# First layer norm of a fused attention and feed-forward block in two token halves, products of zeros ahead of its transposes, Newton steps on GpSimd, and other load and output orders

## The chip, the core and the metric

The kernel runs on one core of a Trainium2 chip. The metric is the device time of one launch in microseconds (us); the time given for a kernel is the median of its runs. Beside the timed runs there is one execution recorded by the hardware profiler, in which every instruction of TensorE (PE; its weight loads are PEld), VectorE (DVE), ScalarE (ACT), GpSimd (POOL) and the DMA queues (SP's above all) has a start and a duration. L12 means line 12 of the kernel file, and lines without a remark are those of the kernel before.

## The reference

x is 16 x 512 x 512 in float32: 16 batches of 512 tokens. Both branches read the same normalised input and are added to x:

```
xn  = (x - mean(x)) / sqrt(var(x) + 1e-5)                # over the last axis
q, k, v = split(xn @ w_qkv.T + b_qkv)                    # 16 heads of 32
att = softmax(causal(q @ k.T / sqrt(32))) @ v
out = x + (att @ w_out.T + b_out)
        + ((silu(xn @ gate_w.T * gate_s) * (xn @ up_w.T * up_s)) @ down_w.T) * down_s   # 512 -> 1408 -> 512
```

gate_w, up_w and down_w hold only -1, 0 and 1.

## The kernel before

**Arithmetic.** Products run in f16. A float32 operand is split into a high half (a cast, mostly on ACT) and a low half (the difference from it, on DVE or POOL), and a product of two such operands is three products: high by high, low by high, high by low. So the 128 x 512 result of a projection with 512 inner elements is twelve matmuls (`mm_group`: four blocks kc of 128 rows, three pairs). The projections' weights wq are staged in float32 and split by `split_wqkv` into wq_h on ACT and wq_l on DVE or, for the first 128 columns of q and of k, in two steps on POOL (L369, L373). The feed-forward weights fit in fp8 exactly, and are loaded as such by GpSimd's DMAs (`load_ffn`, L405; names wg, wu, wd).

**Tiles and loops.** A batch is four token tiles tb of 128 tokens. Its 16 heads are four groups g; batch and group make 64 slots, taken two at a time by `attention_pair`. In a slot PE makes scores s, DVE adds the mask and takes the row maximum (L668), ACT takes the exponential p (L673) and, scaled, pq (L700, and L705 on DVE), a DMA transposes pq to pT, and PE forms av from pT and v. The rest of PE's work (q and k projections `qk_proj` with their copies qkt, qkh, qkl; v; the feed-forward products g, u and dn with ft, hh and hl between them; the output projection op) fills the room between.

**Layer norm.** `ln_load` brings the four x tiles of a batch to xc; `ln_stats` takes mean and variance per token on DVE (L475, L476) and, once for all four tiles, 1/sqrt by two integer operations and three Newton steps of three DVE operations each on 128 x 4 values (`newton_rsqrt`, L33 to L38). `ln_norm` normalises xc (L493). In batches 1 to 15 `ln_turn` casts the result and DMAs transpose it (xnh, xnl to xh, xl). In batch 0 there is no time for this: two tiles are normalised on ACT (L1106, with the shift of L1096) and two on DVE, PE transposes them in sixteen float32 transposes (`ln_tr`, L523) into four PSUM tiles lnT, one per block kc, which ACT casts to xh (L528) and DVE subtracts to xl (L531). The first products of q and k follow.

**Order.** Nothing is issued as the program text has it. Every operation is recorded as a step of `Plan` with its engine, an estimated duration, what it reads and writes, and a slack. `layout` is a list scheduler that lays the steps out by these estimates: on PE by the steps' keys (their places in time, which `Fill.place` gives out; a step may overtake others within AHEAD), on the other engines by the latest time `late` at which a step may start, found backwards from the pass before. `order(6)` makes six passes and takes the shortest. Each engine then executes its instructions in exactly that order (one queue an engine; POOL's and SP's DMA issues lie in the same queues). PSUM and work tiles come from rings (`Tile` with a tag and a number of buffers), and the first user of a buffer waits for the last of the one before. So an edit of one step's engine or estimate also moves steps far from it.

**The start.** x of batch 0 is loaded first, then wq in six pieces: the two pieces of the first 128 columns, the others, and v's two. The planner chooses their order on SP; in the profile a 768 KB piece goes first, and bqk comes after them. `load_ffn` has 35 pieces in all, each waiting for the one two ahead; the first waits for the token "first", which is written with the low halves qkl of group 0.

**The end.** Three quarters of the last batch's output projection are done early (`out_tile` with `upto`), and the rest in two parts, `more`: two products with oh (high half of the attention output) and one with ol. The calls come in this order:

```
for tb in (0, 1, 0, 1, 2, 2, 3, 3):
    ends[tb](f)
```

y is then formed on DVE (L914) and sent out by SP.

## Time and profile before

| | |
|---|---|
| median of 3 timed runs | 1875.51 us (1872.38 to 1876.12) |
| profiled execution | 1874.57 us, of which the span from first to last instruction is 1872.7 us |
| mean clock granted to TensorE | 0.998 of full |
| busy: PE, DVE, ACT, POOL | 1840.9, 1582.0, 1410.6, 966.5 us |
| DMA | 268.94 MB, 144 GB/s |

Busy time is an engine's own work; a step whose operand is not ready holds up all that stands behind it on its engine. In a timeline line the columns are start, busy time, engine, line, operation, output and inputs, shape, how many instructions lie in the group, and in brackets how long the engine was idle ahead of it and what it waited for; a group of matmuls is as long as from its first start to its last end, so that several can overlap. In the view of waits a line says who waited for what: sum in us, times, and the longest. In the windows view the columns are the stretch, its length, each engine's busy time with its instructions, PE's clock, and the DMA engines' share and rate.

### The profile page before, as it was taken

What the parts mean: (1) busy time and instruction counts of PE and PEld (TensorE: products, weight loads), DVE (VectorE), ACT (ScalarE), POOL (GpSimd) and SP (SyncE); (2) the same over time, 40 slices, a digit from 0 to 9 for tenths busy, and PEclk for the clock granted to TensorE, in tenths of its full rate; (3) what the DMA queues carried; (4) which work ended last, traced back from release to release, by engine and by line L of the source; (5) the groups of instructions that cost most, each with busy time, mean ns of one, the idle gap of its engine ahead of it and who ended that gap; (6) DMA issues with size and microseconds to landing.
All of it is one profiled execution on the core that took longest, in us unless ns stands there. A gap on an engine that the chain in (4) does not pass through costs nothing.

```text
span 1872.7 us, 41104 instructions
## 1 busy us (share of the span) xinstructions
PE 1840.9 (98%) x14994; PEld 872.6 (47%) x14994; DVE 1582.0 (84%) x3791; ACT 1410.6 (75%) x3310; POOL 966.5 (52%) x741
## 2 busy tenths in 40 slices
PE   7999999999999999999999999999999999999998
PEld 3444444444444444444444444444444444444443
DVE  6879889889898888979789797897988979787877
ACT  6676877778777787777778777787777877778774
POOL 4654563645645455464645636456363563645543
PEclk9999999999999999999999999999999999999999
DMA  7888676778767688677776867968678786767766
GB/s 163 122 153 168 111 161 142 138 149 144 152 136 143 143 147 154 133 162 135 140 164 129 162 134 127 175 125 164 131 132 167 137 154 128 145 138 140 129 137 131
DMA packets 842545, 268.94 MB, mean 144 GB/s; under 512 B 806496, under 2 KB 813024, under 8 KB 842336
## 3 DMA queue, kind: packets, MB, share of 16 engines
q1 hardware_dynamic: 837296, 264.08, 73.2%
q0 software_dynamic: 5040, 2.16, 1.7%
q8 instruction: 119, 1.95, 0.4%
q14 instruction: 90, 0.74, 0.1%
HBM read 55.59 MB, written 16.78 MB: 39 GB/s over the span
## 4 chain that ended last, share of the span: by engine, by line
PE 85%; DVE 6%; ACT 3%; DMA 2%; POOL 2%; issue 1%; SPq 0%; POOLq 0%; DVEq 0%; ACTq 0%
PE dn L338 15%; PE qk L338 15%; PE u L338 14%; PE g L338 13%; PE op L338 9%; PE v L338 8%; PE s L629 6%; PE av L770 5%; DVE pq L705 2%; ACT p L673 2%; DVE s L668 1%; DMA xl<-xnl 1%; DVE xc L493 1%; POOL xnl L507 1%; DVE ft L860 0%
## 5 line engine op out<-in xcount | busy, mean ns | idle before, releaser
L673 ACT ACTIVATE p<-s,negm 128x512 f32<-128x512 f32 (+3 forms) x1024 | 529.2, 527 | 220.5 <-DVE negm L668 219.2
L668 DVE CUSTOM_DVE_ANT_0 s<-s,mask 128x512 f32<-128x512 f32 (+3 forms) x1024 | 476.5, 515 | 126.2 <-PE s L629 114.4
L705 DVE SCALAR_TENSOR_TENSOR pq<-p,pq 128x1024 f16<-128x1024 f32 (+1 forms) x384 | 491.6, 1301 | 19.9 <-ACT pq L700 15.3
L864 POOL TENSOR_TENSOR hl<-ft,hh 128x512 f16<-128x512 f32 x176 | 245.2, 1394 | 307.5 <-ACT hh L863 284.7
L700 ACT ACTIVATE pq<-p 128x1024 f16<-128x1024 f32 (+1 forms) x384 | 342.0, 915 | 2.9
L338 PE MATMUL u<-xh,wu 128*128 128x512 f16 x704 | 267.3, 380 | 3.7 <-DVE ft L854 3.7
L338 PE MATMUL dn<-wd,hh 128*128 128x512 fp8e4 x704 | 267.2, 380 | 1.8 <-DMA wd<-in_wdT 1.8
L338 PE MATMUL g<-xh,wg 128*128 128x512 f16 x704 | 267.0, 379 | 0.0
L338 PE MATMUL dn<-wd,hl 128*128 128x512 fp8e4 x704 | 266.8, 379 | 0.0
L338 PE MATMUL g<-xl,wg 128*128 128x512 f16 x704 | 266.8, 379 | 0.0
L338 PE MATMUL u<-xl,wu 128*128 128x512 f16 x704 | 266.8, 379 | 0.0
L571 POOL TENSOR_TENSOR qkl<-qkt,qkh 128x512 f16<-128x512 f32 x128 | 171.8, 1344 | 145.9 <-ACT qkh L569 144.3
L338 PEld LDWEIGHTS <-wg 128*128 128x128 fp8e4 x1408 | 135.9, 98 | 168.0 <-issue 6.6
L338 PEld LDWEIGHTS <-wu 128*128 128x128 fp8e4 x1408 | 133.2, 98 | 165.3 <-issue 8.5
L673 ACT ACTIVATION_READ_ACCUMULATOR p<-s,negm 128x1 f32 x1024 | 207.9, 203 | 0.0
L792 POOL TENSOR_SCALAR Rs<-Rs,bv_c 128x512 f32<-128x512 f32 x63 | 100.0, 1587 | 117.3 <-DVE Rs L785 117.3
L566 ACT ACTIVATE qkt<-qk,bqk_c 128x512 f32<-128x512 f32 x128 | 88.1, 689 | 93.0 <-PE qk L338 91.4
L338 PEld LDWEIGHTS <-wq_h 128*128 128x128 f16 x1024 | 99.4, 98 | 124.2 <-issue 7.9
L860 DVE SCALAR_TENSOR_TENSOR ft<-u,gu_c,ft 128x512 f32<-128x512 f32 x176 | 132.0, 750 | 26.0 <-PE u L338 13.7
L854 DVE SCALAR_TENSOR_TENSOR ft<-ft,g 128x512 f32<-128x512 f32 x176 | 119.8, 681 | 32.0 <-ACT ft L850 28.4
L668 DVE DVE_READ_ACCUMULATOR2_ANT negm<- 128x1 f32 x1024 | 144.3, 141 | 0.0
L850 ACT ACTIVATE ft<-g,gt_c 128x512 f32<-128x512 f32 x176 | 120.6, 685 | 31.2 <-PE g L338 30.6
(123 smaller groups left out, 3161.9 us busy)
## 6 DMA issues: line engine op xcount, KB each, us to landing
xc<-in_x SPq DMA_DIRECT2D x64, 256.0 KB, 4.3
xr<-in_x SPq DMA_DIRECT2D x64, 256.0 KB, 2.9
out<-y SPq DMA_DIRECT2D x64, 256.0 KB, 2.3
pT<-pq SPq DMA_TRANSPOSE x384, 4.3
exact<-in_wdT SPq DMA_DIRECT2D x11, 256.0 KB, 2.8
exact<-in_wgT SPq DMA_DIRECT2D x8, 256.0 KB, 3.1
exact<-in_wuT SPq DMA_DIRECT2D x8, 256.0 KB, 2.8
wq<-in_wqkvT SPq DMA_DIRECT2D x2, 768.0 KB, 7.8
```

Of the source, the lines that this page charges most:

```text
L338: nc.tensor.matmul(ps(), l, r, start=(first + k == 0), stop=(first + k == n - 1))
L571: "POOL", gps(512), lambda: nc.gpsimd.tensor_tensor(l(), t(), h(), ALU.subtract),
L629: nc.tensor.matmul(pss[j]()[:, off[u] : off[u] + n], q()[rows, i * P : (i + 1) * P], k()[rows, 0:n], start=(x == 0), stop=(x == 2), tile_p ...
L668: nc.vector.tensor_tensor_reduce(sc, sc, mask[:, 512 - n :], -(2.0 ** -7), 3e38, ALU.add, ALU.min, negm()[:, m : m + 1])
L673: nc.scalar.activation(exps(u).rearrange("p (k j) q -> p k j q", j=4)[:, :, j, :], part().rearrange("p (k q) -> p k q", q=P), AF.Exp, bias ...
L700: "ACT", 0.2 + 0.00085 * n, lambda src=src, half=half: nc.scalar.mul(half(0), src(), 2.0 ** 15),
L705: lambda src=src, half=half: nc.vector.scalar_tensor_tensor(half(1), src(), 2.0 ** 15, half(0), ALU.mult, ALU.subtract),
L792: "POOL", gps(n), lambda: nc.gpsimd.tensor_scalar(r(), r(), bias, None, ALU.add),
L850: "ACT", act(512) + 0.1, lambda: nc.scalar.activation(t(), pg(), AF.Tanh, scale=gt_c[:, ic : ic + 1]),
L854: "DVE", dve(512), lambda: nc.vector.scalar_tensor_tensor(t(), t(), 1.0, pg(), ALU.add, ALU.mult),
L860: lambda: nc.vector.scalar_tensor_tensor(t(), pu(), gu_c[:, ic : ic + 1], t(), ALU.mult, ALU.mult),
L864: add("POOL", gps(512), lambda: nc.gpsimd.tensor_tensor(hl(), t(), hh(), ALU.subtract), r=[t, hh], w=[hl])
```

## The change

There are six edits.

1. `first_row` takes the place of `ln_tr` and of batch 0's statistics and norm. Tiles 0 and 1 are half 0, tiles 2 and 3 half 1, each with its own statistics. Half 0 has its seed on DVE and its Newton steps, as well as the shift, on GpSimd (14 operations of 128 x 2); half 1 does all on DVE. ACT normalises tiles 0, 1 and 3, DVE tile 2. PE transposes tile 0 (four blocks), tile 1 (four), then tiles 2 and 3 block by block.
2. `warm_up` puts 42 matmuls of zeros (128 x 128 by 128 x 384, from the mask's zero columns into a PSUM tile nobody reads) ahead of the transposes and six between tile 1's and the others'.
3. In batches 1 to 15 the seed stays on DVE and the three Newton steps become `newton_steps`, twelve operations on GpSimd; the running minimum vmin is a DVE step of its own.
4. The first 128 columns' wq_l come from DVE like the others. The wq loads and those before are forced into the order of the code (`behind`), bqk after the fourth piece; the planner's estimates of loads change (BEGIN, FIRST_TURN, lat). q's and k's first group are recorded in single matmuls (`piece=1`), so that PE alternates between them.
5. `load_ffn` begins once v's first half piece is loaded, and each piece waits for the one three ahead.
6. The last output parts run as (0, 1, 0, 1, 2, 3, 2, 3), each after the one before.

In the order that the planner then gives, PE's instructions are the same ones apart from those in edits 1 and 2, and from about batch 6 on they also stand in nearly the same order.

```diff
...
+def rsqrt_seed(nc, y, v):
+    yi = y.bitcast(I32)
+    nc.vector.tensor_scalar(yi, v.bitcast(I32), 1, None, ALU.logical_shift_right)
+    nc.vector.tensor_scalar(yi, yi, -1, 0x5F3759DF, ALU.mult, ALU.add)
+
+
+def newton_steps(nc, y, v, t):
+
+    for _ in range(3):
+        nc.gpsimd.tensor_tensor(t, v, y, ALU.mult)
+        nc.gpsimd.tensor_tensor(t, t, y, ALU.mult)
+        nc.gpsimd.tensor_scalar(t, t, -0.5, 1.5, ALU.mult, ALU.add)
+        nc.gpsimd.tensor_tensor(y, t, y, ALU.mult)
+
+
 AHEAD = 20.0
 
 SWITCH, LANDING = 0.095, 1.4
 WINDOW = 0.5
+
+BEGIN, FIRST_TURN = 0.75, 1.3
 
 RUNS = 0.0, 0.17, 0.30, 0.64, 0.80
 LAST_RUNS = 0.0, 0.14, 0.28, 0.42, 0.56
...
-        free = dict.fromkeys(self.ENGINES, 0.0)
+        free = dict.fromkeys(self.ENGINES, BEGIN)
         ready = {e: [] for e in self.ENGINES}
-        made, done, dma, mode = {}, [], 0.0, "wide"
+        made, done, dma, mode = {}, [], FIRST_TURN, "wide"
         keys = sorted((s.key, s.n) for s in self.steps if s.eng == "PE")[::-1]
 
         def begin(st):
 
             t, more = st.at, {}
+            if st.behind and st.behind.end is None:
+                return None
             for b in st.tiles:
                 if b.index is None:
                     l = made.setdefault(b.tag, [])
...
         add(
             "SP", 0.5,
             lambda: nc.sync.dma_start(staged(t, kcs)[:, :, cols], src.rearrange("(k p) f -> p k f", p=P)),
-            w=[(t, k)], lat=4.8 * (cols.stop - cols.start) * (kcs.stop - kcs.start) / 2048,
+            w=[(t, k)], lat=1.6 if cols.stop == P else 3.2 * (cols.stop - cols.start) * (kcs.stop - kcs.start) / 2048,
         )
 
     def split_wqkv(part, k, t, cols, kcs=slice(0, KC)):
...
         dst = slice(part * 512 + cols.start, part * 512 + cols.stop)
         h, l = wq_h[:, kcs, dst], wq_l[:, kcs, dst]
         add("ACT", act(n), lambda: nc.scalar.mul(h, staged(t, kcs)[:, :, cols], 256.0), r=[(t, k)], w=[("wqh", part, k)])
-        if cols.stop == P:
-
-            src = lambda: staged(t, kcs)[:, :, cols]
-            add(
-                "POOL", gps(n), lambda: nc.gpsimd.tensor_scalar(src(), src(), 256.0, None, ALU.mult),
-                r=[(t, k), ("wqh", part, k)], w=[(t, k)],
-            )
-            add(
-                "POOL", gps(n), lambda: nc.gpsimd.tensor_tensor(l, src(), h, ALU.subtract),
-                r=[(t, k), ("wqh", part, k)], w=[("wql", part, k)],
-            )
-            return
         add(
             "DVE", dve(n),
             lambda: nc.vector.scalar_tensor_tensor(l, staged(t, kcs)[:, :, cols], 256.0, h, ALU.mult, ALU.subtract),
...
             for kc in range(KC)
             for nm, dst, src in (("wg", wg, wgT), ("wu", wu, wuT))
         ] + [(wd[:, ic, :], wdT[ic * P : (ic + 1) * P, :], ("wd", ic), 512) for ic in range(IC)]
-        before = ["first", "first"]
+        before = [(wst[3], 1)] * 3
         for dst, src, tok, n in pieces:
             add(
                 "POOL", 0.5, lambda dst=dst, src=src: nc.gpsimd.dma_start(dst, src),
-                r=[before[-2]], w=[tok], lat=0.8 * n / 512,
+                r=[before[-3]], w=[tok], lat=0.8 * n / 512,
             ).dma = True
             before.append(tok)
 
...
 
             add("DVE", 0.8, stat, r=[xc], w=[(bs, tb), (mv, tb)], slack=slack)
 
+        def seed():
+
+            nc.vector.tensor_scalar(v(), mv()[:, :, 1], EPS, 2.0 ** -20, ALU.add, ALU.mult)
+            rsqrt_seed(nc, y(), v())
+
         def rstd():
-
-            nc.vector.tensor_scalar(v(), mv()[:, :, 1], EPS, 2.0 ** -20, ALU.add, ALU.mult)
+            newton_steps(nc, y(), v(), t())
+
+        def least():
             nc.vector.tensor_tensor(vmin, vmin, mv()[:, :, 1], ALU.min)
-            newton_rsqrt(nc, y(), v(), t())
-
-        add("DVE", 2.4, rstd, r=[(mv, tb) for tb in range(NT)], w=[v, y, t], slack=slack)
+
+        add("DVE", 0.5, seed, r=[(mv, tb) for tb in range(NT)], w=[v, (y, 0)], slack=slack)
+        add("POOL", 2.9, rstd, r=[(mv, tb) for tb in range(NT)] + [v, (y, 0)], w=[y, t], slack=slack)
+        add("DVE", 0.08, least, r=[(mv, tb) for tb in range(NT)], w=["vmin"], slack=slack)
 
     def ln_norm(b, tb, slack):
         s = st[b]
...
                 r=[half], w=[(dst, tb)], lat=0.8,
             )
 
...
+    def first_row(f):
+
+        s = st[0]
+        xs, xh, xl = s["xs"], s["xh"], s["xl"]
+        pss = [Tile(pp, [P, 512], F32, "s1", 4, f"lnT_{kc}") for kc in range(KC)]
+
+        def turn(tbs, kcs):
+            def tr():
+                for kc in kcs:
+                    for tb in tbs:
+                        nc.tensor.transpose(
+                            pss[kc]()[:, tb * P : (tb + 1) * P], xs[tb]()[:, kc * P : (kc + 1) * P], ident
+                        )
+
+            f.pe(0.214 * len(tbs) * len(kcs), tr, [xs[tb] for tb in tbs], [(pss[kc], tb) for kc in kcs for tb in tbs])
+
+        for half, pool in ((0, True), (1, False)):
+            nm = f"0_{half}"
+            tile = work("ln_" + nm, "ln0", 2, (P, 24))
+            mv = lambda tile=tile: tile()[:, 0:4].rearrange("p (u n) -> p u n", n=2)
+            bs = lambda tile=tile: tile()[:, 4:16].rearrange("p (u n) -> p u n", n=6)
+            v, y, t, shift = ((lambda tile=tile, k=k: tile()[:, k : k + 2]) for k in (16, 18, 20, 22))
+            tok = lambda *names, tile=tile: [(tile, n) for n in names]
+            eng = nc.gpsimd if pool else nc.vector
+            for u in (0, 1):
+
+                def stat(u=u, mv=mv, bs=bs, xc=xs[2 * half + u]):
+                    nc.vector.bn_stats(bs()[:, u, :], xc())
+                    nc.vector.bn_aggr(mv()[:, u, :], bs()[:, u, :])
+
+                add("DVE", 0.8, stat, r=[xs[2 * half + u]], w=tok(u), slack=-8)
+
+            def seed(mv=mv, v=v, y=y, pool=pool):
+                nc.vector.tensor_scalar(v(), mv()[:, :, 1], EPS, 2.0 ** -20, ALU.add, ALU.mult)
+                if pool:
+                    rsqrt_seed(nc, y(), v())
+
+            def rstd(mv=mv, v=v, y=y, t=t, shift=shift, eng=eng, pool=pool, half=half):
+                (newton_steps if pool else newton_rsqrt)(nc, y(), v(), t())
+
+                eng.tensor_tensor(t(), mv()[:, :, 0], y(), ALU.mult)
+                eng.tensor_scalar(shift(), t(), -1.0, None, ALU.mult)
+
+            def least(mv=mv, half=half):
+                nc.vector.tensor_tensor(
+                    vmin[:, 2 * half : 2 * half + 2], vmin[:, 2 * half : 2 * half + 2], mv()[:, :, 1], ALU.min
                 )
 
-        f.pe(0.45, tr, s["xs"], [ps])
-        add("ACT", act(512), lambda: nc.scalar.copy(xh()[:, kc, :], ps()), r=[ps], w=[(xh, kc)], slack=-8)
-        add(
-            "DVE", dve(512),
-            lambda: nc.vector.tensor_tensor(xl()[:, kc, :], ps(), xh()[:, kc, :], ALU.subtract),
-            r=[ps, (xh, kc)], w=[(xl, kc)], slack=-8,
-        )
+            add("DVE", 0.5 if pool else 0.2, lambda fn=seed: fn(), r=tok(0, 1), w=tok("seed"), slack=-8)
+            add(
+                "POOL" if pool else "DVE", 2.9 if pool else 2.6, lambda fn=rstd: fn(), r=tok(0, 1, "seed"),
+                w=tok("y"), slack=-8,
+            )
+            add("DVE", 0.08, lambda fn=least: fn(), r=tok(0, 1), w=["vmin"], slack=5)
+            for u in (0, 1):
+                xc = xs[2 * half + u]
+                if not pool and u == 0:
+                    add(
+                        "DVE", 0.5,
+                        lambda xc=xc, mv=mv, y=y: nc.vector.tensor_scalar(
+                            xc(), xc(), mv()[:, 0, 0:1], y()[:, 0:1], ALU.subtract, ALU.mult
+                        ),
+                        r=[xc] + tok(0, "y"), w=[xc], slack=-8,
+                    )
+                else:
+                    add(
+                        "ACT", act(512) + 0.1,
+                        lambda u=u, xc=xc, shift=shift, y=y: nc.scalar.activation(
+                            xc(), xc(), AF.Identity, bias=shift()[:, u : u + 1], scale=y()[:, u : u + 1]
+                        ),
+                        r=[xc] + tok("y"), w=[xc], slack=-8,
+                    )
+        warm_up(f, 42)
+        turn((0,), range(KC))
+        turn((1,), range(KC))
+        warm_up(f, 6)
+        for kc in range(KC):
+            turn((2, 3), (kc,))
+        for kc, ps in enumerate(pss):
+            toks = [(ps, tb) for tb in range(NT)]
+            add(
+                "ACT", act(512), lambda kc=kc, ps=ps: nc.scalar.copy(xh()[:, kc, :], ps()), r=toks, w=[(xh, kc)],
+                slack=-8,
+            )
+            add(
+                "DVE", dve(512),
+                lambda kc=kc, ps=ps: nc.vector.tensor_tensor(xl()[:, kc, :], ps(), xh()[:, kc, :], ALU.subtract),
+                r=toks + [(xh, kc)], w=[(xl, kc)], slack=-8,
+            )
+
+    warm = Tile(pp, [P, 512], F32, "av", 1, "warm")
+
+    def warm_up(f, n):
+
+
+        def run():
+            for _ in range(n):
+                nc.tensor.matmul(warm()[:, 0:384], mask[:, 0:P], mask[:, 0:384], start=True, stop=True)
+
+        f.pe(1.5 + 0.161 * n if n > 20 else 0.161 * n, run, [], [warm])
 
...
-            late=0 if b or g else 8,
+            late=0 if b or g else 11, piece=4 if b or g else 1,
         )
...
             return finish()
         steps = iter([(0, 2), (2, 3)])
 
-        def more(f):
-
-            nonlocal last
+        def more(f, after):
+
             k0, k1 = next(steps)
-            last = mm_group(f, ps, ops([upto])[k0:k1], first=3 * upto + k0, n=3 * NG, after=last)
+            after = mm_group(f, ps, ops([upto])[k0:k1], first=3 * upto + k0, n=3 * NG, after=last + after)
             if k1 == 3:
                 finish()
+            return after
 
         return more
 
...
     pieces += [(2, k, wst[2 + k], both, slice(2 * k, 2 * k + 2)) for k in range(2)]
     for n, piece in enumerate(pieces):
         load_wqkv(*piece)
-        if n == 1:
+        if n == 3:
             add("SP", 0.5, lambda: nc.sync.dma_start(bqk_c, bqk), w=["bqk"], lat=0.3)
-    ln_stats(0, -8)
-    shift = work("shift", "rden", 2, (P, 16))
-    mv, y = st[0]["mv"], st[0]["ln"][1]
-    add(
-        "DVE", 0.2,
-        lambda: nc.vector.scalar_tensor_tensor(shift()[:, 0:NT], mv()[:, :, 0], -1.0, y(), ALU.mult, ALU.mult),
-        r=[(mv, tb) for tb in range(NT)] + [y], w=[shift], slack=-8,
-    )
-    for tb in range(NT):
-        if tb % 2 == 0:
-            ln_norm(0, tb, -8)
-            continue
-        xc = st[0]["xs"][tb]
-        add(
-            "ACT", act(512),
-            lambda tb=tb, xc=xc: nc.scalar.activation(
-                xc(), xc(), AF.Identity, bias=shift()[:, tb : tb + 1], scale=y()[:, tb : tb + 1]
-            ),
-            r=[xc, shift, y], w=[xc], slack=-8,
-        )
-
+    loads = [step for step in plan.steps if step.dma]
+    for before, step in zip(loads, loads[1:]):
+        step.behind = before
...
     f = Fill()
-    for kc in range(KC):
-        ln_tr(f, 0, kc)
+    first_row(f)
     for which in (0, 1):
         qk_proj(f, 0, 0, which)
     f.place(0.0, f.total)
...
             count_good(when, start - 0.6 * T)
     av_step(NB - 1, NG - 1, start - 0.3 * T)
     f = Fill()
-    for tb in (0, 1, 0, 1, 2, 2, 3, 3):
-        ends[tb](f)
+    after = []
+    for tb in (0, 1, 0, 1, 2, 3, 2, 3):
+        after = ends[tb](f, after)
     f.place(start, f.total)
```

More of the change, by code (lines that the diff above doesn't have):

```diff
@@ L72, in __init__ @@
         self.end = self.late = None
+        self.behind = None
 class Plan:
@@ L464, in ln_load @@
                 "SP", 0.5, lambda tb=tb, xc=xc: nc.sync.dma_start(xc(), x[b, tb * P : (tb + 1) * P, :]),
-                r=when, w=[xc], lat=0.85,
+                r=when, w=[xc], lat=0.85 if b else 1.05,
             )
@@ L513, in ln_turn @@
             )
-    def ln_tr(f, b, kc):
-        s = st[b]
-        ps = Tile(pp, [P, 512], F32, "s1", 4, f"lnT_{b}_{kc}")
-        xh, xl = s["xh"], s["xl"]
-        def tr():
-            for tb in range(NT):
-                nc.tensor.transpose(
-                    ps()[:, tb * P : (tb + 1) * P], s["xs"][tb]()[:, kc * P : (kc + 1) * P], ident
-                )
-        f.pe(0.45, tr, s["xs"], [ps])
-        add("ACT", act(512), lambda: nc.scalar.copy(xh()[:, kc, :], ps()), r=[ps], w=[(xh, kc)], slack=-8)
-        add(
-            "DVE", dve(512),
-            lambda: nc.vector.tensor_tensor(xl()[:, kc, :], ps(), xh()[:, kc, :], ALU.subtract),
-            r=[ps, (xh, kc)], w=[(xl, kc)], slack=-8,
-        )
+    def first_row(f):
[34 more added lines that the diff above has]
+                    vmin[:, 2 * half : 2 * half + 2], vmin[:, 2 * half : 2 * half + 2], mv()[:, :, 1], ALU.min
+                )
+            add("DVE", 0.5 if pool else 0.2, lambda fn=seed: fn(), r=tok(0, 1), w=tok("seed"), slack=-8)
[39 more added lines that the diff above has]
+            )
@@ L1088, in fast_path @@
         load_wqkv(*piece)
-        if n == 1:
+        if n == 3:
             add("SP", 0.5, lambda: nc.sync.dma_start(bqk_c, bqk), w=["bqk"], lat=0.3)
-    ln_stats(0, -8)
-    shift = work("shift", "rden", 2, (P, 16))
-    mv, y = st[0]["mv"], st[0]["ln"][1]
-    add(
-        "DVE", 0.2,
-        lambda: nc.vector.scalar_tensor_tensor(shift()[:, 0:NT], mv()[:, :, 0], -1.0, y(), ALU.mult, ALU.mult),
-        r=[(mv, tb) for tb in range(NT)] + [y], w=[shift], slack=-8,
-    )
-    for tb in range(NT):
-        if tb % 2 == 0:
-            ln_norm(0, tb, -8)
-            continue
-        xc = st[0]["xs"][tb]
-        add(
-            "ACT", act(512),
-            lambda tb=tb, xc=xc: nc.scalar.activation(
-                xc(), xc(), AF.Identity, bias=shift()[:, tb : tb + 1], scale=y()[:, tb : tb + 1]
-            ),
-            r=[xc, shift, y], w=[xc], slack=-8,
-        )
+    loads = [step for step in plan.steps if step.dma]
+    for before, step in zip(loads, loads[1:]):
+        step.behind = before
     def scale_bqk():
```

## The prediction

> **What bounds the kernel now.** I read the engine table of the page first, then the windows view of a long middle stretch.
>
> ```profile
> PE 1840.9 (98%) x14994; PEld 872.6 (47%) x14994; DVE 1582.0 (84%) x3791; ACT 1410.6 (75%) x3310; POOL 966.5 (52%) x741
> 60.00:1800.00 1740.00, 1728.66 (x14172) 819.46 (x14172) 1484.76 (x3545) 1324.78 (x3117) 910.86 (x673) 1.00 0.76 144
> ```
>
> PE is busy 1840.9 of 1872.7 us and holds 99.3% of the middle stretch. The change takes no product away, so it can only win PE's 31.8 idle us, or stretches at a lower clock. Third, the waits on PE:
>
> ```profile
> PE lnT L523 <- DVE xc L493: 11.0, 1, 11.0
> PE u L338 <- DVE ft L854: 3.7, 4, 1.5
> PE s L629 <- ACT p L673: 3.6, 5, 1.0
> PE dn L338 <- DMA wd<-in_wdT: 1.8, 1, 1.8
> PE qk L338 <- POOL wq_l L373: 1.2, 1, 1.2
> ```
>
> Eleven us stand before the first transpose, the rest in single waits; the same view cut to 60 to 170 us has most of those on ft and p and the one on wd. So I read, fourth, the timeline of the start:
>
> ```profile
> 7.62 0.18 DVE L476 BATCH_NORM_AGGREGATE mv<-bs 128x2 f32<-128x6 f32 x1
> 8.45 0.16 DVE L36 SCALAR_TENSOR_TENSOR ln_t<-ln_v,ln_y 128x4 f32<-128x4 f32 x1
> 8.64 0.16 DVE L37 TENSOR_TENSOR ln_t<-ln_t,ln_y 128x4 f32<-128x4 f32 x1
> 10.42 1.52 ACT L1106 ACTIVATE xc<-xc,shift,ln_y 128x512 f32<-128x512 f32 x2 [4.86 <-DVE shift L1096]
> 10.99 4.04 PE L523 MATMUL lnT<-ident,xc 128*128 128x128 f32 x16 [10.99 <-DVE xc L493]
> 14.82 1.64 PE L338 MATMUL qk<-xh,wq_h 128*128 128x512 f16 x4
> 15.06 0.59 ACT L528 CAST xh<-lnT 128x512 f16<-128x512 f32 x1 [0.27 <-PE lnT L523]
> 16.30 1.03 PE L338 MATMUL qk<-xl,wq_h 128*128 128x512 f16 x4
> 21.97 1.04 PE L338 MATMUL qk<-xh,wq_l 128*128 128x512 f16 x4 [1.19 <-POOL wq_l L373]
> 27.16 1.03 PE L338 MATMUL v<-wq_h,xh 128*128 128x512 f16 x4
> ```
>
> The reader is to see the chain (statistics, Newton steps on four columns, norm, transpose, cast, products) and that the first four products take 1.64 us where later ones take 1.03: the clock is low until about 16. The 48 products of q and k end at about 26.95.
>
> **The start, part by part.** The forecast is a chain of rows in the new order. Half 0 needs two of the four statistics: these end at 5.30 by the rows (5.12 and 0.18); three seed steps at the Newton pitch of 0.20 end at 5.9. Then 14 GpSimd operations of 2 columns. No row has one so small. Their bounds: 0.18 each, a memset's 0.10 and the 0.08 that separates the dependent GpSimd pair at 14.15 (1.52 after 12.55); and 0.50, the 0.53 memset of 512 elements almost whole. I take 0.23: 0.15, near a DVE Newton step's 0.16, which with four columns is fixed cost and not elements either, plus the 0.08; and 0.8 once for meeting DVE's instructions. That ends at 5.9 + 3.2 + 0.8 = 9.9. ScalarE meanwhile loads its table (no longer behind x) and makes the first high weights once they land. Norms of x0, x1, x3 on ScalarE at the row's 0.76 pitch end at 10.75, 11.45, 12.2; x2 comes from DVE by 11.6.
>
> The 48 products of zeros are 1/4 shorter than a 512-wide one: 0.75 x 0.216 = 0.162 warm, 0.32 cold. [...] Transposes, 0.213 apart while cold where nothing waits (the sixteen in 4.04), go at half, 0.107. Those of x1 end at 11.9, six more zeros (0.97) at 12.9, and the four turns of x2 and x3 feed casts that end from 14.0 to 15.7, against 15.65 before. So the last cast is not earlier: ACT carries three norms, a weight piece and four casts in a row. The gain lies behind it: the products start warm (4 x 0.21 = 0.8 saved), run q and k in turn, so none waits for a whole row, and the 1.2 wait for wq_l goes because DVE makes it in one step in place of GpSimd's 2.53 and 1.66. Of the 48 products 24 are done by 19.6, and the others, 24 x 0.216 = 5.2, by 24.8: **2.1 us** earlier than 26.95. Next late there is qkt, which ends near 21.6, before v is through.
>
> Bounds: with 0.50 per GpSimd step the chain is 3.8 later, and x2 and x3 wait less than x0, so I count 2.9 of it: 0.8 lost. With 0.18, no interplay and all loads early, 3.5 gained.
>
> [...]
>
> Six feed-forward loads now leave GpSimd right after the values' weights are under way instead of at 27.23: six issues at 0.55 (the L405 rows) lie ahead of GpSimd's first qkl. They land about 0.63 apart before, so 3.8 us of transfer can delay the last wq piece from 15.99 to 19.8; ScalarE reaches it at about 19.8. I count nothing, 1 us if that cover is gone.
>
> **The wait on wd.** All wd issues now stand ahead of group 3's qkl and of all but the first of batch 1's four xnl; before, the last was issued at 110.60 behind an xnl that waited 5.97, and landed at 114.15. The 1.8 us on PE goes; next late would be hl, whose GpSimd rows start at 111.19, hence 1.0 to 2.0: **1.8**.
>
> **Newton steps of batch 1.** Here they decide something:
>
> ```profile
> 59.54 1.15 POOL L571 TENSOR_TENSOR qkl<-qkt,qkh 128x512 f16<-128x512 f32 x1 [1.08 <-issue]
> 59.67 1.04 DVE L36 SCALAR_TENSOR_TENSOR ln_t<-ln_v,ln_y 128x4 f32<-128x4 f32 x1
> 60.75 1.09 DVE L37 TENSOR_TENSOR ln_t<-ln_t,ln_y 128x4 f32<-128x4 f32 x1
> 63.68 2.75 DVE L493 TENSOR_SCALAR xc<-xc,mv,ln_y 128x512 f32<-128x512 f32 x4
> 70.55 0.39 PE L629 MATMUL s<-qkh,qkh 32*128 32x384 f16 x1 [0.35 <-ACT p L673]
> ```
>
> and, from the windows view of the stretch behind it (the column with 0.50 is PE's clock):
>
> ```profile
> 70.70:74.00 3.30, 3.30 (x27) 1.56 (x20) 2.73 (x6) 3.21 (x5) 2.84 (x3) 0.50 0.20 40
> ```
>
> A DVE step of 0.16 takes 1.04 while GpSimd works. The chain (59.08 to 62.62), a pq product of 1.22 and the four norms put the row maxima off; PE stalls about 2.6 us around 68 to 70.55 and then runs 3.4 us at half clock, which loses about 1.6: 4.2 in all. After the change, the twelve GpSimd steps run beside pq: 12 x 0.23 + 1.0 = 3.8 from 59.1, so the norms start at 62.9 instead of 63.68. [...] I take **1.0**.
>
> [...]
>
> **Batches 2 to 15.** The Newton steps (9 x 0.2 on DVE, 1.8 a batch) leave an engine that PE does not wait for, and the GpSimd chain of about 3 to 5 us has cover: in the new order DVE does 4 to 6 us between seed and norm in batches 2 to 5, about 7.2 after (two pq at 1.22, ft 0.68 and 0.75, eight row maxima at 0.42). Zero. If the cover is gone, DVE stands at the norm and the maxima behind it are late.
>
> **The tail.** In pairs, op_2 and op_3 end last; the y rows (four from 1864.07, 0.60 apart) need op_2 by 1865.3: 0.1 later. The out transfers follow.
>
> **Sum.** 2.1 (start) + 1.8 (wd) + 1.0 (batch 1) - 0.1 (tail): 4.8 less. The profiled execution took 1874.57 (span 1872.7 and 1.9 around it), 0.94 under the median 1875.51. So 1869.8 there, and **1870.7** as a median. A change under 0.2%, 3.75 us, this kernel's times can't tell from none.
>
> **Rivals.** More gain (0.17): the early stalls on ft and p (6.3 us on PE, batches 1 and 2) go too, since the order there changes and DVE has 1.8 more a batch; 2.3 to 5.3 more, 1865.4 to 1868.4. Against it: those waits follow ft and maxima that stay on DVE.
>
> No difference (0.17): the start gives nothing, by slow GpSimd steps or because loads collide, and early stalls re-form at other places; what is left is wd's 1.8 against up to 2 new, 1873.5 to 1877. For it: 60 to 170 us already holds most of PE's waits and all orders there move.
>
> Slower (0.12): one mechanism, GpSimd's steps stretched by DVE.
>
> ```profile
> L864 POOL TENSOR_TENSOR hl<-ft,hh x176: 1147/1159/2155, 48.2 to 1833.1; 128x512 f16<-128x512 f32 x176
> ```
>
> The same operation takes 1.16 or up to 2.16, one us more when it meets DVE. If small steps also pay this, each pq can hold one up. From a mean step of 0.6 (7.2 over 12) the norm of every steady batch is late, and each tenth more costs 12 x 0.1 = 1.2 us on DVE in 14 batches, of which PE feels perhaps half: +4 to +20, 1879 to 1895. Against it: most of the 176 are at 1.16, and there are two pq in a cover, so 2 us of stretch and not 12.
>
> **Numbers.** The forecast, 1868.5 to 1873, has 0.54: three quarters of it (0.39) is beyond 3.75, the rest within. With more gain's 0.17: faster 0.56; same 0.15 + 0.17 = 0.32; slower 0.12. The range 1866 to 1876 takes in the forecast, nearly all of more gain and most of no difference.
>
> **What would show it.** Right: the first real transpose near 10.8 with pitch 0.107, v's first product near 25, no wait on wd, GpSimd steps at 0.2 to 0.3, the batch-1 norm by 63 less the start's gain, PE's middle busy share unchanged. Wrong: zeros still running when x0 is ready, GpSimd steps over 0.6, DVE idle before the norms of steady batches, or new stalls on p in 60 to 170 us.

## The result: 12.3 us less, and the profile after

The changed kernel takes 1863.07 us (median of 6 runs, 1861.75 to 1865.63) where the kernel before, beside it, took 1875.35: a ratio of 0.9937, 95% interval 0.9924 to 0.9950. The forecast had 1870.7 and a range from 1866 to 1876. The direction was right; the gain was two and a half times the forecast and 2.9 us beyond the range. The profiled execution took 1861.75 (span 1860.0), 12.8 less than the one of before.

First the engine table, a middle stretch from the windows view, and all waits on PE, for the kernel after.

```profile
PE 1844.9 (99%) x15042; PEld 876.0 (47%) x15042; DVE 1547.7 (83%) x3662; ACT 1412.1 (76%) x3311; POOL 999.6 (54%) x931
```

```profile
60.00:1800.00 1740.00, 1734.24 (x14215) 822.81 (x14208) 1456.64 (x3438) 1334.94 (x3142) 946.77 (x856) 1.00 0.67 145
```

```profile
PE s L726 <- ACT p L770: 4.5, 5, 3.7
PE warm L628 <- POOL vmin L314: 1.5, 1, 1.5
PE u L359 <- DVE ft L951: 1.1, 2, 0.6
PE op L359 <- ACT oh L900: 1.1, 1, 1.1
```

PE's 11.0 us before the first transpose are filled with zeros from 1.48 on, the waits on wd and wq_l are gone and that on ft is down from 3.7 to 1.1. The wait on p grew, from 3.6 with 1.0 as the longest to 4.5 with 3.7. In the middle stretch PE is busy for 5.6 us more (1734.24 against 1728.66). The forecast had 2.8 of it, the wait on wd and 1.0 at batch 1's stall.

The start, from the timeline after:

```profile
1.48 10.12 PE L628 MATMUL warm<-mask 128*128 128x384 bf16 x48 [1.48 <-POOL vmin L314]
6.11 0.20 POOL L50 TENSOR_TENSOR ln<-ln 128x2 f32<-128x2 f32 x1 [4.07 <-DVE ln L44]
6.38 0.20 POOL L51 TENSOR_TENSOR ln<-ln 128x2 f32<-128x2 f32 x1
9.76 0.23 POOL L572 TENSOR_SCALAR ln<-ln 128x2 f32<-128x2 f32 x1
10.03 2.22 ACT L598 ACTIVATE xc<-xc,ln 128x512 f32<-128x512 f32 x3 [1.69 <-POOL ln L572]
11.44 1.91 PE L541 MATMUL lnT<-ident,xc 128*128 128x128 f32 x16
12.73 2.05 ACT L612 CAST xh<-lnT 128x512 f16<-128x512 f32 x4
13.37 1.84 PE L359 MATMUL qk<-xh,wq_h 128*128 128x512 f16 x7
23.89 1.03 PE L359 MATMUL v<-wq_h,xh 128*128 128x512 f16 x4
```

A GpSimd step on 128 x 2 takes 0.20, one every 0.28. The chain ends at 9.99 (forecast 9.9), the norms start at 10.03, sixteen transposes take 1.91 us instead of 4.04, the last cast ends at 14.78 instead of 15.65, and v's first product is at 23.89 instead of 27.16. In the executed order all 48 zeros stand ahead of the transposes (one row, up to 11.60). The first transpose starts at 11.44; where the zeros are not issued (below), it starts at 10.71. So the zeros were still running for about 0.7 us when x0 was ready. The first 14 zeros, up to 5.90, take 0.32 each, the others 0.16; the transposes take 1.91 behind them and 3.68 where no zeros are issued. The clock column of the windows view reads 1.00 for both stretches, as it does for 10.99 to 16.06 in the kernel before. So what the rows show at the start is durations; the low clock there, and its rise, of which the prediction and the expectations speak, were inferred from them and are not shown.

Batch 1, from the timeline after, and behind it two rows of the windows view:

```profile
59.32 1.11 POOL L50 TENSOR_TENSOR ln_t<-ln_v,ln_y 128x4 f32<-128x4 f32 x1 [1.21 <-DVE ln_y L44]
63.33 0.20 POOL L53 TENSOR_TENSOR ln_y<-ln_t,ln_y 128x4 f32<-128x4 f32 x1
63.56 5.91 DVE L509 TENSOR_SCALAR xc<-xc,mv,ln_y 128x512 f32<-128x512 f32 x4 [3.11 <-POOL ln_y L53]
71.00 0.47 PE L726 MATMUL s<-qkh,qkh 32*128 32x384 f16 x1 [3.72 <-ACT p L770]
```

```profile
70.00:74.00 4.00, 2.41 (x22) 0.98 (x22) 3.88 (x11) 3.80 (x10) 0.66 (x1) 0.59 1.33 170
74.00:78.00 4.00, 4.00 (x20) 1.53 (x13) 3.90 (x10) 2.71 (x5) 3.99 (x4) 0.55 0.53 100
```

The steps now end at 63.53, DVE stands idle for 3.11 us, and its four norms take 5.91 us where they took 2.75. PE stands 3.72 in one piece and then works at a low clock, which the two windows up to 78 give as 0.59 and 0.55 (0.50 from 71.5 to 76). A second profiled execution of the changed kernel (same_chip_after, below) has the same stall of 3.72 and the same norms of 5.91.

**Where the time went.** Three stalls of the kernel before, from its timeline, that are gone after:

```profile
90.96 0.38 PE L338 MATMUL u<-xh,wu 128*128 128x512 f16 x1 [1.46 <-DVE ft L854]
103.51 1.31 PE L629 MATMUL s<-qkh,qkh 32*128 32x256 f16 x4 [0.94 <-ACT p L673]
147.88 0.38 PE L338 MATMUL u<-xh,wu 128*128 128x512 f16 x1 [1.54 <-DVE ft L854]
```

The whole, from the starts of the same products in both traces (negative: earlier after):

| place | drift, us |
|---|---|
| v's first product (27.16, 23.89) | -3.3 |
| score products near 39 that waited | -0.8 |
| batch 1's stall and half clock (gate product 65.98 to 61.92 ahead of it, 85.02 to 84.64 behind it) | +3.7 |
| stalls on ft at 89 and on p at 102 to 104, gone | -3.6 |
| wait on wd at 112, gone | -2.0 |
| stall on ft at 146, gone | -1.7 |
| small waits | +0.7 |
| batch 1's first v product (159.14, 152.18) | -7.0 |
| from there to batch 15's (1764.97, 1752.69) | -5.3 |

The second execution of the changed kernel has +3.0 at batch 1's stall, -8.2 at batch 1's first v product and -4.4 from there to batch 15's, so a single row holds to about 1 us.

### The profile page after: what moved, and what is told of

It reads as the page before. It is cut to its first block, busy times and chain, and to the rows that moved or that the text cites. A ratio compares the mean times of both kernels' runs of the same rounds, so it can differ in the third digit from the quotient of the medians.

```text
span 1860.0 us, 41219 instructions
## 1 busy us (share of the span) xinstructions
PE 1844.9 (99%) x15042; PEld 876.0 (47%) x15042; DVE 1547.7 (83%) x3662; ACT 1412.1 (76%) x3311; POOL 999.6 (54%) x931
## 4 chain that ended last, share of the span: by engine, by line
PE 94%; DVE 3%; ACT 2%; issue 1%; POOL 1%; DVEq 0%; ACTq 0%; POOLq 0%
PE qk L359 17%; PE u L359 16%; PE dn L359 16%; PE g L359 15%; PE v L359 9%; PE op L359 9%; PE s L726 6%; PE av L867 6%; DVE pq L802 1%; ACT p L770 1%; PE warm L628 1%; DVE s L765 1%; ACT pq L797 0%; DVE xc L509 0%; DVE ft L957 0%
## 5 line engine op out<-in xcount | busy, mean ns | idle before, releaser
L802 DVE SCALAR_TENSOR_TENSOR pq<-p,pq 128x1024 f16<-128x1024 f32 (+1 forms) x384 | 470.9, 1247 | 37.8 <-ACT pq L797 30.2
L961 POOL TENSOR_TENSOR hl<-ft,hh 128x512 f16<-128x512 f32 x176 | 240.1, 1366 | 248.3 <-ACT hh L960 245.6
```

What stands on the lines that cost most here:

```text
L802: lambda src=src, half=half: nc.vector.scalar_tensor_tensor(half(1), src(), 2.0 ** 15, half(0), ALU.mult, ALU.subtract),
L961: add("POOL", gps(512), lambda: nc.gpsimd.tensor_tensor(hl(), t(), hh(), ALU.subtract), r=[t, hh], w=[hl])
```

## The experiments

Each kernel ran beside the kernel before. The table holds the median, the ratio to the kernel before with its 95% interval, and how far v's first product of batches 0, 1 and 15 has moved against the kernel before in the profiled executions, us. Executions of one kernel differ by up to 9.7 us (the kernel before, 1872.64 to 1882.36), and the median of the kernel before moved from 1873.63 to 1875.80 between the groups of runs, so differences of a us or two between rows, and small shifts late in a trace, are not read.

Three theories of the gain that was not forecast stand behind the expectations. A: DVE has 1.8 us less to do in each batch. B: the feed-forward loads. C: the order alone, since the planner makes another one with every edit.

| run | median | ratio | batch 0 | batch 1 | batch 15 |
|---|---|---|---|---|---|
| changed kernel | 1863.07 | 0.9937 (0.9924 to 0.9950) | -3.3 | -7.0 | -12.3 |
| before_loads_early | 1864.36 | 0.9939 (0.9921 to 0.9956) | +0.2 | -8.8 | -9.9 |
| before_loads_moved_only | 1872.73 | 0.9988 (0.9978 to 0.9999) | -0.4 | -3.1 | -2.1 |
| before_loads_start | 1873.48 | 0.9992 (0.9982 to 1.0002) | -0.1 | -3.7 | -0.3 |
| before_loads_chain3 | 1866.63 | 0.9961 (0.9950 to 0.9973) | -0.5 | -8.2 | -7.8 |
| after_loads_late | 1869.58 | 0.9968 (0.9955 to 0.9980) | -3.3 | -3.0 | -5.9 |
| before_estimates | 1873.72 | 0.9998 (0.9989 to 1.0008) | +0.1 | -0.9 | +1.1 |
| before_start_alone | 1874.65 | 1.0003 (0.9993 to 1.0013) | -3.6 | +1.6 | -2.1 |
| after_zeros_not_issued | 1862.05 | 0.9942 (0.9924 to 0.9959) | -1.6 | -7.5 | -12.0 |
| after_no_zeros | 1858.93 | 0.9927 (0.9911 to 0.9944) | -1.4 | -10.4 | -15.4 |
| after_half0_dve | 1864.47 | 0.9952 (0.9935 to 0.9968) | +7.1 | -4.8 | -9.0 |
| before_newton_pool | 1878.53 | 1.0009 (0.9998 to 1.0020) | +1.0 | +4.2 | +3.3 |
| after_newton_dve | 1860.82 | 0.9916 (0.9899 to 0.9932) | -3.0 | -9.5 | -13.4 |
| after_newton_dve_frozen | 1866.35 | 0.9961 (0.9947 to 0.9975) | -2.6 | -9.2 | -8.3 |
| after_b1_newton_dve | 1860.96 | 0.9929 (0.9912 to 0.9945) | -2.8 | -8.9 | -13.3 |
| best_no_zeros_newton_dve | 1865.71 | 0.9958 (0.9944 to 0.9973) | -1.1 | -12.2 | -9.0 |
| best_no_zeros_b1_dve | 1859.91 | 0.9924 (0.9906 to 0.9941) | -0.5 | -8.7 | -13.5 |
| same_chip_after | 1862.09 | 0.9930 (0.9915 to 0.9946) | -3.5 | -8.2 | -12.6 |
| same_chip_no_zeros | 1858.41 | 0.9911 (0.9895 to 0.9927) | -1.0 | -9.1 | -14.1 |

### The feed-forward loads

**The loads alone, on the kernel before.**

```diff
-        before = ["first", "first"]
+        before = [(wst[3], 1)] * 3
...
-                r=[before[-2]], w=[tok], lat=0.8 * n / 512,
+                r=[before[-3]], w=[tok], lat=0.8 * n / 512,
```

> The kernel before with edit 5 alone: feed-forward loads begin after v's first half piece of wq and go three at a time. Theory A: only the wd wait goes, 1873.5. Theory B: wd and the stalls at 89, 102 and 146 go, about 1868; the later ones stay. Theory C: anything from 1868 to 1877.

More than theory B's number: 1864.36, 11.4 less than the kernel before beside it and nearly the whole change. Its waits on PE:

```profile
PE lnT L523 <- DVE xc L493: 11.2, 1, 11.2
PE s L629 <- ACT p L673: 2.9, 7, 0.8
PE u L338 <- DVE ft L854: 2.4, 3, 1.1
PE qk L338 <- POOL wq_l L373: 1.6, 1, 1.6
```

The start is the old one; wd is gone and no wait on p is over 0.8. **The loads late again, in the changed kernel:**

```diff
-        before = [(wst[3], 1)] * 3
+        before = ["first", "first"]
...
-                r=[before[-3]], w=[tok], lat=0.8 * n / 512,
+                r=[before[-2]], w=[tok], lat=0.8 * n / 512,
```

> The changed kernel with edit 5 undone: feed-forward loads begin with group 0's low halves and go two at a time. Theory A (DVE's time): 1863 plus the wait on wd, 1865; stalls at 89, 102 and 146 stay away. Theory B (GpSimd's loads): these come back, 2 on wd and 5 on ft and p, about 1870. Theory C (order): between these, at other places.

It loses 6.5 us. That is theory B's number, but not by theory B's stalls: PE waits 4.3 for wg in one piece and 1.1 for wd, and the waits on ft and p stay small.

```profile
PE g L359 <- DMA wg<-in_wgT: 4.3, 1, 4.3
PE u L359 <- DVE ft L951: 2.0, 5, 0.6
```

Is it the transfers or the order? **The loads moved only** keeps the old order and puts the issues in GpSimd's queue where the run with the loads alone has them (`early` lists these places):

```diff
     done = plan.order(6)
...
+    loads = [p for p in done if p.eng == "POOL" and p.dma]
+    rest, done, n = [p for p in done if not (p.eng == "POOL" and p.dma)], [], 0
+    for p in rest:
+        while loads and early[len(early) - len(loads)] <= n:
+            done.append(loads.pop(0))
+        done.append(p)
+        n += p.eng == "POOL"
```

> The kernel before in its own order on PE, DVE, ACT and SP and of GpSimd's arithmetic; only the 35 feed-forward load issues stand earlier in GpSimd's queue, where the run with early loads alone has them. It tells the two readings of that run (-11.4 us) apart. Theory B1, the loads' own timing: late weights and issues in GpSimd's way are what holds p and ft up, so most of the gain is here too, 1864 to 1867. Theory B2, the planner: with weights planned earlier it puts gate and up products where PE would wait, and the order does it; here only the wd wait goes, and a little may be lost where issues now delay low halves: 1872 to 1876, stalls at 39, 68 to 70, 89, 102 and 146 still there.

B2 holds: 2 us. The wd wait goes; the stall on ft near 90 goes too, which B2 did not have, and a stretch at a clock of 0.76 (the window from 100 to 106) gives about as much back. The stalls on p near 70 and 101 and on ft near 145 stay. So about 9 us of the 11.4 are the order's. In the timelines the last up weights are issued at 77.88 in the kernel before and at 58.39 and 58.57 in the two others. But the batch-1 stall differs. First its first score product, in the kernel before and in the run with the order planned for early loads, and that run's fourth norm; then the waits of the run with the loads moved only:

```profile
67.96 0.32 PE L629 MATMUL s<-qkh,qkh 32*128 32x384 f16 x1
70.69 0.74 PE L629 MATMUL s<-qkh,qkh 32*128 32x384 f16 x3
72.20 0.54 DVE L493 TENSOR_SCALAR xc<-xc,mv,ln_y 128x512 f32<-128x512 f32 x1
```

```profile
PE s L629 <- ACT p L673: 4.7, 7, 0.9
PE u L338 <- DVE ft L854: 2.0, 3, 1.4
```

With early weights the planner puts one more gate and one more up group (16 products, 3.5 us) ahead of this score group: PE comes to it at 70.69 instead of 67.96 and waits 0.35 for p. On DVE the fourth norm stands behind the row maxima, at 72.20, where the kernel before has it ahead of them, at 65.05. **Half of the edit each:**

```diff
-        before = ["first", "first"]
+        before = [(wst[3], 1)] * 2
```

> The kernel before with half of edit 5: the loads begin after v's first half piece, but each still waits for the one two ahead. If the early start is what counts: 1864 to 1867. If the third load in flight is: 1872 to 1876.

```diff
-        before = ["first", "first"]
+        before = ["first"] * 3
...
-                r=[before[-2]], w=[tok], lat=0.8 * n / 512,
+                r=[before[-3]], w=[tok], lat=0.8 * n / 512,
```

> The kernel before with the other half of edit 5: loads begin with group 0's low halves as before, but three at a time. The early start alone left batch 1's v 3.7 us earlier (both halves together 8.8) and the end level. If the third load in flight is what lets the planner place gate and up products in time: batch 1's v 4 to 8 us earlier, 1867 to 1872. If only both together do: batch 1's v 0 to 3 earlier, 1871 to 1876.

The third load in flight carries most of it (batch 1's v -8.2; 1866.63, 7.2 less than the kernel before beside it). The early start alone moves batch 1's v by 3.7, and its order gives that back later, at a ft wait of 2.3 us and others. It has the same 16 products ahead of the score group, and PE still waits 2.0 for p there, because the norms are late: a DVE operation of 0.17 took 3.12 beside two load issues and two operations of GpSimd.

```profile
63.81 3.12 DVE L34 TENSOR_SCALAR ln_y<-ln_y 128x4 int32<-128x4 int32 x1
```

What the early start would give without this collision was not tested.

**Is any other order as good?**

```diff
-        free = dict.fromkeys(self.ENGINES, 0.0)
+        free = dict.fromkeys(self.ENGINES, 0.75)
...
-        made, done, dma, mode = {}, [], 0.0, "wide"
+        made, done, dma, mode = {}, [], 1.3, "wide"
```

> The kernel before with nothing but two of the planner's numbers changed (engines begin at 0.75, loads at 1.3 us). No instruction differs, only the order. Theory C (any edit moves stalls by chance): 2 to 6 us either way, 1869 to 1881, the steady stalls at 1137 and 1483 replaced by others. If order moves little by itself: within 1.5 us of before, stalls in place.

This run does not answer it. In its trace the instructions of every engine, and SP's transfers, stand in the same order as in the kernel before: the two numbers changed no order, so it is the same order measured once more. What speaks against chance is the table. Two other orders planned for the kernel before without edit 5, before_newton_pool and before_start_alone, gain nothing. The seven orders planned with three loads in flight have batch 1's v 4.8 to 12.2 earlier, the four others planned anew with two in flight from 3.7 earlier to 4.2 later. Why the order is the better one is shown for batch 1's stall only.

### The start

**Edits 1, 2 and 4 alone** (the changed kernel with its loads, Newton steps of batches 1 to 15 and tail put back).

```diff
...
-        add("DVE", 0.5, seed, r=[(mv, tb) for tb in range(NT)], w=[v, (y, 0)], slack=slack)
-        add("POOL", 2.9, rstd, r=[(mv, tb) for tb in range(NT)] + [v, (y, 0)], w=[y, t], slack=slack)
+        add("DVE", 2.4, rstd, r=[(mv, tb) for tb in range(NT)], w=[v, y, t], slack=slack)
...
-        before = [(wst[3], 1)] * 3
+        before = ["first", "first"]
...
-    for tb in (0, 1, 0, 1, 2, 3, 2, 3):
+    for tb in (0, 1, 0, 1, 2, 2, 3, 3):
...
```

> Edits 1, 2 and 4 alone (two halves, zeros, weights' order and wq_l on DVE), with the kernel before's loads, Newton steps of batches 1 to 15, and tail. The start was forecast at 2.1 us and measured 3.3 at v's first product. If that passes to the end: batch 1's v 3 earlier and 1871 to 1873. If batch 1's stall takes it back (beside early loads the start moved batch 1's v by only 9.5 - 8.8 = 0.7): batch 1's v 0 to 1.5 earlier, the stall near 68 us longer by 2 to 3, 1873 to 1876.

v's first product is 3.6 us earlier, batch 1's is 1.6 later, and the time is 1874.65: nothing arrives. Its waits on p are longer than before, one of 2.9 at 103.50 among them:

```profile
PE s L719 <- ACT p L763: 5.5, 4, 2.9
```

Beside early loads (after_newton_dve has edits 1, 2, 4 and 6 more than before_loads_early) batch 1's v is only 0.7 earlier as well; the end is 3.5 earlier, which comes from later batches, and the intervals of the two ratios overlap. **Zeros planned but not issued:**

```diff
-            for _ in range(n):
+            for _ in range(0):
```

> The changed kernel in its own order, planned with the zeros but without issuing them; so it differs by the clock of the first products alone, where the run without zeros also had another order. Expected: transposes and first products slow as in that run, v's first product 1.5 to 2.5 later than 23.89. If that passes to the end: 1864.5 to 1866. If batch 1's stall absorbs it (DVE's chain there sets the time): batch 1's v within 0.7 of the changed kernel's and 1862.5 to 1864; then the gain of 4 in the run without zeros was the order's.

The transposes take 3.68 us, v's first product is 1.7 later, and the time is that of the changed kernel. The zeros' effect on the first products is worth 1.7 us there and nothing at the end, since batch 1's norms (4.84 here, 5.91 with zeros) and its clock (from 70 to 74 and from 74 to 78, 1.00 and 0.57 here, 0.59 and 0.55 with zeros) give it back. **Without zeros in the plan too:**

```diff
-        warm_up(f, 42)
...
-        warm_up(f, 6)
```

> The changed kernel without the 48 products of zeros. If they bring the start's gain (v's first product at 23.89 instead of 27.16) by the clock: transposes at 0.213 again (16 x 0.107 = 1.7) and the first products of q and k at 0.43 until the clock rises, v's first product at 26 to 27 and 1865 to 1867. If the halves, the weights' order and q and k in turn bring it: v's first product at 24.0 to 24.7, 1863 to 1864.5.

Neither expectation: 4 us under the changed kernel. In this order GpSimd's chain (4.3 against 4.2) and the norms beside GpSimd's work (5.32 against 5.91) are much alike, but DVE comes to batch 1's norms earlier:

```profile
60.98 5.32 DVE L509 TENSOR_SCALAR xc<-xc,mv,ln_y 128x512 f32<-128x512 f32 x4 [2.55 <-POOL ln_y L53]
```

They end at 66.3 instead of 69.5, PE waits 1.3 for p there instead of 4.3, and its clock stays at 1.00 from 66 to 78. Both on one chip:

> The changed kernel itself, on one chip with the run beside it, since the variants that came out 2 to 4 us under it ran on other chips than it did. If the chips agree: 1862 to 1864.

> The changed kernel without zeros on the same chip. If the 4 us are the kernel's and not the chip's: 1858 to 1860, and no run of one as long as a run of the other. If they are the chip's: within 1 us of the changed kernel.

1862.09 (1861.36 to 1863.38) and 1858.41 (1857.22 to 1861.12), six runs each that do not overlap. So this version beats both kernels: 0.9911 of the kernel before, interval 0.9895 to 0.9927. (after_newton_dve, at 0.9916, was not run beside it.) **Half 0 on DVE:**

```diff
-        for half, pool in ((0, True), (1, False)):
+        for half, pool in ((0, False), (1, False)):
```

> The changed kernel with half 0's Newton steps and shift on DVE instead of GpSimd (there 6.11 to 9.98). If GpSimd's place in parallel with the second half's statistics is worth something: DVE does both halves in turn, 2 x 2.3 us behind the statistics, the norms start 1 to 2 later than 10.03 and v's first product is at 24.5 to 25.5. If the loads and casts set the start: v's first product stays within 0.4 of 23.89.

This one did not test what it was made for. With GpSimd free, the feed-forward loads leave at 1.75 us, and wq comes late: the first wq_h starts at 11.40 instead of 7.71.

```profile
1.75 0.78 POOL L414 DMA_DIRECT2D wg<-in_wgT  x1
```

The planner's wait for v's weights is no wait on the chip; in the changed kernel the Newton steps ahead of the issues in GpSimd's queue hold the loads back (the first leaves at 9.95, right behind the operation at 9.76). v's first product is 10.4 us later than in the changed kernel, and the end only 1.4.

### The Newton steps

**On GpSimd in the kernel before** (edit 3 alone), and **on DVE in the changed kernel** (edit 3 undone, the lines below the other way round), planned anew, without the helper functions in the diff:

```diff
...
-        add("DVE", 2.4, rstd, r=[(mv, tb) for tb in range(NT)], w=[v, y, t], slack=slack)
+        add("DVE", 0.5, seed, r=[(mv, tb) for tb in range(NT)], w=[v, (y, 0)], slack=slack)
+        add("POOL", 2.9, rstd, r=[(mv, tb) for tb in range(NT)] + [v, (y, 0)], w=[y, t], slack=slack)
+        add("DVE", 0.08, least, r=[(mv, tb) for tb in range(NT)], w=["vmin"], slack=slack)
```

> The kernel before with edit 3 alone: Newton steps of batches 1 to 15 on GpSimd. Theory A: 8 us less than before (1867), the later stalls gone. Theory B: as before, 1875, with batch 1's stall up to 4 longer, so up to 1879. Theory C: 1867 to 1879, stalls at new places; the steady ones at 1137 and 1483 may go or be replaced.

> The changed kernel with edit 3 undone: Newton steps of batches 1 to 15 back on DVE, planned anew. Three theories of where the unforeseen 8 us went (stalls on ft and p at 89, 102 and 146 us of the kernel before, and those at 439, 607, 1137 and 1483). Theory A, DVE has 1.8 us more a batch: without that they come back, so about 1871, start still 3.3 early. Theory B, GpSimd's early loads: they stay away, and batch 1's stall shrinks from 5.9 to about 4 because no norm waits for GpSimd, so 1860 to 1862. Theory C, the order alone (the planner makes another order with every edit, and stalls come and go with it): anything between 1859 and 1871, with stalls at new places.

Edit 3 is no gain in either: 1878.53 with it (batch 1's wait on p grows to 4.5 in one piece), where the interval of the ratio still holds 1, and 1863.07 with it against 1860.82 without, where the two intervals overlap. Theory A, which had the early stalls vanish by DVE's relief, falls: with the Newton steps back on DVE the changed kernel's longest waits on p and ft are 0.9 and 0.4. **In the changed kernel's own order**, only the issuing engine changed, for batch 1 and, without the condition, for batches 1 to 15 (`newton_dve` has the nine DVE operations of `newton_rsqrt`):

```diff
-            newton_steps(nc, y(), v(), t())
+            (newton_dve if b == 1 else newton_steps)(nc, y(), v(), t())
```

> The changed kernel in its own order, but batch 1's nine Newton operations are issued on DVE where the order has GpSimd's twelve. The changed kernel's stall at 67 to 72 us is 5.9 us against 4.2 before. If GpSimd's chain (4.2 us, DVE idle 3.1 of it) and the norms that collide with GpSimd's work behind it (5.91 for four instead of 2.75) cause that, the norms end 3 to 5 us earlier, and the time is 1859 to 1861. If the stall is the order's (row maxima behind the norms): 1862.5 to 1863.5.

> The changed kernel in its own order, with the Newton operations of batches 1 to 15 issued on DVE at the same places. Planned anew with them on DVE it took 1860.8, with batch 1's alone on DVE 1861.0. If GpSimd's Newton steps cost only where the norm waits (batch 1): 1860.5 to 1861.5. If their place costs in every batch: below 1860. If DVE's 1.8 us a batch was worth something: 1862 to 1866, with stalls on p or ft in the middle.

Batch 1's alone halves the stall, to 1.9 in one piece, and brings batch 1's v forward by 1.9 against one execution of the changed kernel and by 0.7 against the other. At the end no gain is shown: 1860.96, and the interval of its ratio overlaps with both of the changed kernel's. Its norms, from the timeline of that run, take 2.75 again, with no idle DVE ahead:

```profile
65.33 2.75 DVE L516 TENSOR_SCALAR xc<-xc,mv,ln_y 128x512 f32<-128x512 f32 x4
```

The others', in the same order, cost 5.4 us (1866.35 against 1860.96): there DVE's time counts after all, and an order planned for GpSimd's Newton steps needs it. Planned anew, the kernel does without. The two attempts to add up gains are told by the table:

> The changed kernel without zeros and with the Newton steps of batches 1 to 15 on DVE, planned anew: the two undone edits that were faster each (1858.9 and 1860.8). If their gains add: 1856 to 1858. If both gained by the same thing, batch 1's stall: 1858 to 1861.

> The changed kernel without zeros, planned as in that run, with batch 1's Newton steps alone issued on DVE. If GpSimd's chain delays batch 1's norms there too: 1856.5 to 1858.5, stall at 68 us (1.9 on PE) gone or halved. If the stall is already hidden there: 1858.5 to 1859.5.

The first takes the zeros' two lines and edit 3 out of the changed kernel, the second the zeros' two lines, with batch 1's Newton steps issued on DVE. They do not add. Without zeros and with Newton on DVE, batch 1's v is earliest of all (-12.2), and an order with a ft wait of 2.3 us and others in the later batches spoils it. Without zeros, batch 1's stall is hidden already.

## Why the prediction was wrong in size

**The loads** were the failing step. I sized their edit by the one wait that bears a load's name: 1.8 us for wd (measured 2.0), and counted the six early issues at nothing. The loads were also what the planner ordered gate and up products by. Alone they gave 11.4 on the kernel before, of which moving the issues in the old order gave 2.1, and 6.5 of the changed kernel's time depends on them. The stalls at 89, 102 and 146 that went have ft and p as their releasers. The rival "more gain" had them go for two reasons: another order, which is what the runs show, though it did not name the loads, and DVE's relief, which is not the cause. Its range, 1865.4 to 1868.4, was too small as well.

**The start** was right as a chain (3.3 for 2.1, since the weights and casts came earlier than I had them), and wrong in being carried to the end. Alone it gives nothing. That the GpSimd chain ended at 9.99 for 9.9 is luck in part: a step costs 0.28 and not 0.23, and the 0.8 counted for meeting DVE did not come. One sign of being wrong came: the zeros were still running when x0 was ready. They cost 0.7 there; with them v's first product is still 1.7 earlier.

**Batch 1** had the wrong sign: 1.0 of gain was forecast, for norms that start at 62.9 instead of 63.68, and 3.7 of loss came. A new stall on p between 60 and 170, one of the signs of being wrong, is the one at 71.00. Two terms: a step costs 0.28 and not 0.23, with 0.9 for meeting pq as forecast, which makes the chain 4.2 for 3.8; and the norms behind it run into GpSimd's work and take 3.2 longer, which I had not looked at. About 2 of the 3.7 are the engine: the same place costs 1.3 in after_b1_newton_dve, against 3.7 and 3.0 in two executions of the changed kernel. The cause of the rest stays open. The start alone loses 5.2 between batch 0's v and batch 1's too, but mostly at other waits (1.6 at 78, 2.9 at 103.50, 1.8 at 159).

**Batches 2 to 15** at zero: the chain was hidden as forecast (DVE waits for GpSimd ahead of a norm only once in the trace, in batch 1). DVE's 1.8 a batch are worth 5.4 us in the order made for them, against nothing in an order planned without; the 5.3 us of the trace (4.4 in the second execution) are thus the order's and the engine's together, and how they share it in the kernel before is not settled.

**The tail** was right: DVE's four y take 2.58 instead of 2.48, and PE's new wait of 1.1 on oh costs no more than that. The slower rival did not come: steps at 0.28 stay under the 0.6 from which it decides.

## What to carry to other kernels

Where a planner orders the work, an edit of when an operand may be there is to be priced by what the planner does with it, not by the wait that bears its name: build the order and see which products stand ahead of each stall. A gain ahead of a stage whose own chain ends later is not carried to the end; look for the next place where the engine waits for something that did not move. And an order and an engine are to be tested apart, by issuing the same order with one thing changed. A run that is meant as another order is one only if the order in its trace differs.

## What the runs showed of the chip

DVE's norm of 128 x 512 takes 0.54 alone (median 0.535 before), 1.35 beside a GpSimd subtraction, and once 2.79 where two load issues and another GpSimd operation lay beside it. In the line below, of the kernel after, the columns are shortest, median and longest, ns:

```profile
L509 DVE TENSOR_SCALAR xc<-xc,mv,ln_y x60: 528/813/2789, 63.6 to 1674.1; 128x512 f32<-128x512 f32 x60
L50 POOL TENSOR_TENSOR ln_t<-ln_v,ln_y x45: 195/200/1114, 59.3 to 1667.7; 128x4 f32<-128x4 f32 x45
```

GpSimd's small steps pay it as well, 1.11 instead of 0.20 beside pq, once in the batch-1 chain and not at each step. Why is not shown. A small step comes every 0.28 on GpSimd (kernel after) and every 0.20 on DVE (kernel before); a whole Newton step is four operations on GpSimd and three on DVE, 1.12 against 0.60.

A wait that only the planner knows does not bind the chip: in after_half0_dve, with nothing ahead of them in GpSimd's queue, the loads planned behind v's weights left at 1.75 us, before wq's first issue at 2.62, and the first wq_h started at 11.40 instead of 7.71.
